# A fallback branch moved from the middle of a recurrence-and-attention kernel to its end, with larger residual fetches and shifted statistics

## The chip, the cores and the metric

The kernel runs on one core of a Trainium2 chip. The metric is the device time of one execution in microseconds (us). Five engines take part: TensorE (PE in the profile), VectorE (DVE), ScalarE (ACT), GpSimd (POOL) and SyncE (SP, which only issues transfers). Each runs its own list of instructions in order, and semaphores make one wait for another.

## The reference, cut to what matters

Everything is float32. `x` has the shape (2, 2048, 256).

```
xi = layernorm(x) @ Wi.T + bi
h_t = tanh(xi_t + h_(t-1) @ Wh.T + bh)          # recurrence over t = 0..2047
x = x + h
y = layernorm(x)
q, k = y @ Wq, y @ Wk                           # 8 heads of 64
wv = top2mask(y @ Ws) * sigmoid(y @ Ws)         # 5 experts per head
v = sum over e of wv[.., e] * (y @ Wv[e])
attn = softmax(q @ k.T / 8) @ v
out = x + sum over h, e of top2mask(y @ Wd) * attn @ Wo[e]
```

The recurrence is sequential over 2048 steps. The kernel does not run it so: it cuts time into 128 segments of 16 steps and treats the segments as columns of one matrix.

## The kernel before, in words

**Recurrence.** `run("a", True, ...)` goes through the steps 3 to 15 of all segments at once, from a zero state, and leaves each segment's last state in `ends`. `run("b", False, ...)` goes through the 16 steps again, each segment starting from its left neighbour's end. If the ends of run b equal those of run a (to a tolerance of four units of 2^-23), the result holds. Beside run b, `beside(s)` turns the states of earlier steps back (`turn_back`, L385), adds them to `x` (`add_back`, L394, which also stores the sum to the DRAM tensor `x1d`), and takes the statistics of the second layer norm of batch 0 (`stats_back`, L399).

**The check and the branch (L503 to L535).** Right behind run b, DVE compares the ends (L505 to L510: four instructions), one matmul sums the count over partitions (`pc`, L515) and DVE writes the integer `again` (L520). `nc.values_load` (L521) makes all five engines read it into a register, and `tc.If(flag > 0)` (L522) branches on it. The body of the branch repeats the recurrence until it must have closed; with the inputs of the test it is skipped. Code on one side of the branch can't be mixed with code on the other.

**Between branch and attention (L537 to L548).** `stats_back(S - 1)`, `roots` (a Newton iteration of small DVE instructions), the normalisation of the second half of batch 0 (`norm_back`, four on DVE and four on POOL), then on PE `queries(0, 0)`, `logits(0)`, `keys(0, 0)`, `logits(4)` and the transposes `turn_norm`.

**Attention.** 16 pairs of batch and head, four blocks of 512 queries each: 64 units. A unit takes four steps T, so T runs from 0 to 255; each step handles two tiles of 256 keys by 512 queries. PE multiplies (`scores`, L636), ACT copies the scores to an SBUF ring (`stage`, L648), DVE keeps a running maximum (`largest`, L658). At the unit's end PE transposes the maximum (`turn_max`), DVE reduces it (`reduce_max`, mq, L682), and PE spreads it again (`spread_max`, pt, L691). Some steps later POOL or DVE subtracts it (L704), ACT takes the exponential (L707), PE multiplies by v (`products`, L717), POOL's transfer queue folds pairs of tiles (`fold`, L729, an accumulating transfer), and PE sums them (`sums`, L738). `close` and `gather` weigh and store a head's output in `yd`; for the last head `fetch_y` (L804) reads it back and POOL adds (L840). `turn_out` (L848) transposes a chunk of 128 rows and fetches its residual `z` from `x1d` (L862, 128 KB, three buffers); `project_out` (L865) multiplies by Wo, DVE adds `z` (L878), SP stores it (L879).

**Order of the work.** Inside `tc.manual_schedule()` every engine takes its instructions in program order. Within a step the order is written out in the loop from L1127; what is not part of the fixed step hangs in the tables `before` (ahead of `products`) and `behind` (at the step's end), filled from L939 to L1025. Batch 1 is normalised there, late: `load_late` (L884), `stats_late` (L888): for each unit from the fourth on, a pair of chunks has both statistics at the end of the unit's last step (L983). `drain` (L1027) is the hand-written order behind the last step: it transposes the last 14 and projects and stores the last 15 of the last batch's 16 chunks while the last two units finish.

**The end.** When the program's last transfers are issued, SP waits for their semaphores and all engines meet (L1223).

Of the kernel before, what the change touches and what calls it, by code (L numbers as in the profile page):

```python
# [8 lines left out]
F32 = mybir.dt.float32  # L9
# [8 lines left out]


@with_exitstack  # L20
def rnn_then_switchhead_kernel(
    ctx: ExitStack,
    tc: tile.TileContext,
    x: bass.AP,
# [8 lines left out]
    Wv: bass.AP,  # L33
    Wo: bass.AP,
    out: bass.AP,
):
    nc = tc.nc
    B, T, D = x.shape
    E, _, DH = Wv.shape
    H = Wq.shape[1] // DH  # L40
# [7 lines left out]
    HE = H * E  # L48
    SCALE = float(DH) ** -0.5

    const = ctx.enter_context(tc.tile_pool(name="const", bufs=1))
    keep = ctx.enter_context(tc.tile_pool(name="keep", bufs=1))
    early = ctx.enter_context(tc.tile_pool(name="early", bufs=1))

    rw = ctx.enter_context(ExitStack())
    rconst = rw.enter_context(tc.tile_pool(name="rconst", bufs=1))
# [4 lines left out]
    dram = ctx.enter_context(tc.tile_pool(name="dram", bufs=1, space=bass.MemoryType.DRAM))  # L63
    x1d = dram.tile([NCH, P, B, D], F32, name="x1d")
    yd = dram.tile([B, T // 512, P, 4, E, DH], F32, name="yd")
    xvd = dram.tile([B, NCH // 4, P, 4, DH, E], F32, name="xvd")

    def load_x(c):
        nc.sync.dma_start(
# [48 lines left out]
    ps_m = ctx.enter_context(tc.tile_pool(name="ps_m", bufs=2, space=PSUM))  # L118

    def misc(shape, nm):  # L120
        return ps_m.tile(shape, F32, tag="m", name=nm)
# [136 lines left out]
    NEWTON = 3  # L258


    rst = rw.enter_context(tc.tile_pool(name="rst", bufs=1))
    xi = rst.tile([P, KC, S, B, NS], F32, name="xi")
    hs = rst.tile([P, KC, S, B, NS], F32, name="hs")

# [2 lines left out]
    nc.gpsimd.memset(ends, 0.0)  # L267
    nc.gpsimd.memset(ones, 1.0)

    with tc.tile_pool(name="prep", bufs=3) as pp, tc.tile_pool(  # L270
        name="lna", bufs=3
    ) as lnp, tc.tile_pool(name="ps_xi", bufs=3, space=PSUM) as ps_xi, tc.tile_pool(
        name="ps_t", bufs=3, space=PSUM
    ) as ps_t, tc.manual_schedule():
        norm_of, turned = {}, {}
# [61 lines left out]

    TOL = 4 * 2.0**-23  # L340
    GC = NCH // 2
    SKIP = 3
    EARLY = S - 1
    sp = rw.enter_context(tc.tile_pool(name="step", bufs=3))
    lnp = rw.enter_context(tc.tile_pool(name="ln", bufs=2))
    ps_t = ctx.enter_context(ExitStack())
    pst = ps_t.enter_context(tc.tile_pool(name="ps_tb", bufs=2, space=PSUM))
    mv2 = [sp.tile([P, GC, 2], F32, tag=f"mv{g}", bufs=1, name=f"mvb{g}") for g in range(2)]
    hv_of, root_of = {}, {}

# [144 lines left out]
                )  # L495
        nc.scalar.copy(gates_all[:, c0 : c0 + 4, 0, :], pg)

    with tc.tile_pool(name="ps_h", bufs=1, space=PSUM) as ps_h:

        with tc.manual_schedule():  # L500
            run("a", True, False, ps_h)
            run("b", False, True, ps_h, beside)
            N = KC * B * NS  # L503
            off = sp.tile([P, KC, B, NS], F32, tag="off", bufs=1, name="off")
            nc.vector.tensor_tensor(off, hs[:, :, S - 1], ends[:, :, :, 1:], ALU.subtract)  # L505
            good = sp.tile([P, KC, B, NS], F32, tag="good", bufs=1, name="good")
            nc.vector.tensor_scalar(good, off, TOL, None, ALU.is_le)
            nc.vector.scalar_tensor_tensor(good, off, -TOL, good, ALU.is_ge, ALU.mult)
            count = sp.tile([P, 1], F32, tag="count", bufs=1, name="count")
            nc.vector.tensor_reduce(count, good.rearrange("p c b n -> p (c b n)"), AX.X, ALU.add)  # L510
            turn_back(S - 1, "b")
            for c in range(0, GC, 2):
                turn_norm(c, xn_of.pop(c), "b")
            pc = misc([1, 1], "pc")
            nc.tensor.matmul(pc, lhsT=count, rhs=ones, start=True, stop=True)  # L515
            for c in (S - 2, S - 1):
                add_back(c, nc.vector)
            stats_back(EARLY - 1, "b")
            again = sp.tile([1, 1], I32, tag="again", bufs=1, name="again")
            nc.vector.tensor_scalar(again, pc, float(P * N) - 0.5, None, ALU.is_lt)  # L520
        flag = nc.values_load(again[0:1, 0:1], min_val=0, max_val=1)  # L521
        with tc.If(flag > 0):  # L522
            for c in range(S):
                load_x(c)
            with tc.For_i(0, NS - 1, 1):
                nc.vector.tensor_copy(ends[:, :, :, 1:], hs[:, :, S - 1])
                run("c", False, True, ps_h)
            for c in range(S):
                turn_back(c, "c")
                add_back(c, nc.gpsimd)  # L530
                if c < EARLY:
                    stats_back(c, "c")
            *_, root_of[0] = roots(mv2[0], GC, "c")
            for c in range(0, GC, 2):
                turn_norm(c, norm_back(c, "c", pool2), "c")  # L535

    with tc.manual_schedule():  # L537

        stats_back(S - 1, "d")
        *_, root_of[1] = roots(mv2[1], GC, "d")  # L540
        for c in range(GC, S, 2):
            xn_of[c] = norm_back(c, "d", (nc.vector, nc.gpsimd))
        queries(0, 0)
        logits(0)
        keys(0, 0)
        logits(4)
        for c in range(GC, S, 2):
            turn_norm(c, xn_of.pop(c), "d")  # L548
# [8 lines left out]
    U_T = NCH // 4  # L557
    LAG = U_T + 2
    RING = (LAG + 4, LAG + 3)
    big = ctx.enter_context(tc.tile_pool(name="big", bufs=1))  # L560
    ap = ctx.enter_context(tc.tile_pool(name="attn", bufs=2))
    four = ctx.enter_context(tc.tile_pool(name="four", bufs=1))
    ps_o = ctx.enter_context(tc.tile_pool(name="ps_o", bufs=1, space=PSUM))
    scores_only = ctx.enter_context(ExitStack())
    ps_s = scores_only.enter_context(tc.tile_pool(name="ps_s", bufs=2, space=PSUM))
# [282 lines left out]
    def turn_out(b, c):  # L848
        yf = y_of[b, c // QS][:, c % QS].rearrange("p e k -> p (e k)")
        py = other(f"py{b}_{c}")[:, : len(o_chunks) * P] if spare else misc([P, len(o_chunks) * P], f"py{b}_{c}")  # L850
        py = py.rearrange("p (k n) -> p k n", n=P)
        for k, (r0, m) in enumerate(o_chunks):
            nc.tensor.transpose(py[0:m, k, :], yf[:, r0 : r0 + m], ident)  # L853
        yT = yT_all[yT_of["n"] % 2]
        yT_of["n"] += 1
        full = sum(m == P for _, m in o_chunks)
        nc.scalar.copy(yT[:, 0:full, :], py[:, 0:full, :])  # L857
        for k, (r0, m) in enumerate(o_chunks):
            if m < P:
                nc.scalar.copy(yT[0:m, k, :], py[0:m, k, :])  # L860
        z = ap.tile([P, D], F32, tag="z", bufs=3, name=f"z{b}_{c}")
        nc.sync.dma_start(out=z, in_=x1d[c, :, b, :])  # L862
        yT_of[b, c] = (yT, z)

    def project_out(b, c, at_end=False):  # L865
        yT, z = yT_of.pop((b, c))
# [69 lines left out]
        late["c"].pop(0)()  # L936


    before, first_behind, behind = {}, {}, {}  # L939

    def at(table, T, f, *a):
        table.setdefault(T, []).append(lambda: f(*a))
# [34 lines left out]
    for b in range(1, B):  # L977

        T0 = (b - 1) * H * H_T + 2 * LAG + 3
        for c in range(NCH):  # L980
            T = T0 + c // 2 * U_T
            at(behind, T - 2 + c % 2, load_late, b, c)
            at(behind, T, stats_late, b, c)  # L983
        T0 += NCH // 2 * U_T
        for part in range(2):
            at(behind, T0 + 3, scales_late, b, part)
            T0 += U_T
        for c in range(NCH):
# [12 lines left out]
        assert T0 <= b * H * H_T  # L1001
# [25 lines left out]
    def drain():  # L1027
# [13 lines left out]
        def project(n=1):  # L1041
            nonlocal projected
            for _ in range(n):
                project_out(*outs[projected])
                projected += 1

        spread_max(v)
        turn_max(u)
        subtract(tv + 6, True)
# [22 lines left out]
        products(tv + 7)  # L1072
        fold(tv + 6)
        turn()
        project()
        take(v)
        sums(tv, tv + 2, True, False)
        exponential(tu + 2)
# [47 lines left out]
    with tc.manual_schedule():  # L1126
        for T in range(NT):  # L1127
# [49 lines left out]
        assert not before and not behind and not first_behind  # L1177
        scores_only.close()
        spare["pool"] = ctx.enter_context(tc.tile_pool(name="ps_z", bufs=4, space=PSUM))
        drain()  # L1180


# [44 lines left out]
```

## Time and profile before

| what | value |
|---|---|
| three runs, median (lowest to highest) | 1567.89 us (1567.87 to 1571.04) |
| the profiled execution itself | 1569.4 us |
| its span, first to last instruction | 1567.6 us |
| mean granted TensorE clock | 0.997 |
| PE busy | 1512.6 us, 96% |
| DVE, POOL, ACT busy | 1299.1, 1287.7, 1247.8 us |

The stages, read from the timeline of each engine: the input side and both runs of the recurrence reach to about 114 us; check, branch and the first projections to about 130 us; attention from there to about 1512 us; the drain to the end. The profile shows, for each group of instructions, where it is in the code, what it writes and reads, how long one takes, and what ended the idle time of its engine before it. "issue" means that the engine waited for nothing that the profile shows. An entry such as PEldq or SPq is an engine's sequencer: waits on semaphores, register loads, branches.

### The profile page before, as it was taken

How to read it: one execution, taken by the hardware profiler on the slowest of the kernel's cores; microseconds unless marked ns; L12 is line 12 of the kernel's file. 1: busy time of each engine (PE TensorE's matmuls, PEld its weight loads, DVE VectorE, ACT ScalarE, POOL GpSimd, SP SyncE). 2: the span in 40 equal slices, each digit the busy share in tenths (PEclk: the TensorE clock that was granted, in tenths of full speed). 3: DMA queues.
4: the chain of work that ended last, by engine and by line, in shares of the span. 5: the costliest groups of instructions: out<-in, count | busy, mean ns of one | idle time of the engine just before them, and what ended most of it. 6: DMA issues, size and time to landing. Idle time of an engine off the chain costs nothing. (4 is left out here: it accounts for less than half of the span.)

```text
span 1567.6 us, 41503 instructions
## 1 busy us (share of the span) xinstructions
PE 1512.6 (96%) x17582; PEld 533.7 (34%) x17582; DVE 1299.1 (83%) x1811; ACT 1247.8 (80%) x1617; POOL 1287.7 (82%) x855
## 2 busy tenths in 40 slices
PE   6988899999999999999999999999999999999997
PEld 5984222222233333333223332222222222222233
DVE  7473799999988888888987779999999999999873
ACT  4674688888888888888887778888888888888882
POOL 3053699898999988999998778899999999999980
PEclk9999999999999999999999999999999999999999
DMA  5021377888889987888897767788888888888955
GB/s 167 1 109 32 102 153 189 186 187 176 181 174 188 177 180 161 173 171 175 171 202 155 163 159 181 170 178 179 176 179 178 176 176 170 176 174 176 197 117 149
DMA packets 86959, 254.09 MB, mean 162 GB/s; under 512 B 11952, under 2 KB 31216, under 8 KB 86768
## 3 DMA queue, kind: packets, MB, share of 16 engines
q0 software_dynamic: 43488, 164.65, 57.5%
q1 hardware_dynamic: 41648, 86.13, 16.5%
q8 instruction: 139, 2.28, 0.6%
q10 hardware_dynamic: 1632, 0.61, 0.1%
q14 instruction: 52, 0.43, 0.1%
HBM read 59.46 MB, written 50.33 MB: 70 GB/s over the span
## 5 line engine op out<-in xcount | busy, mean ns | idle before, releaser
L704 POOL TENSOR_TENSOR p<-p,top 128x1024 f32<-128x1024 f32 x378 | 1006.3, 2768 | 27.9 <-ACT top L697 27.4
L648 ACT COPY p<-s 128x1024 f32<-128x1024 f32 x512 | 511.7, 1013 | 139.8 <-issue 49.5
L707 ACT ACTIVATE p<-p 128x1024 f32<-128x1024 f32 x512 | 538.8, 1063 | 50.7 <-DVE p L704 41.9
L636 PE MATMUL s<-q,k 64*32 64x512 f32 x4096 | 501.6, 596 | 3.6 <-ACT p L648 2.4
L636 PE MATMUL s<-qs,k 64*32 64x512 f32 x4096 | 501.4, 596 | 3.3 <-ACT p L648 1.8
L717 PE MATMUL o<-p,v 128*32 128x512 f32 x4096 | 491.0, 597 | 3.2 <-DVE os L754 2.3
L658 DVE TENSOR_TENSOR m<-s,m 128x1024 f32<-128x1024 f32 x320 | 390.9, 1222 | 89.4 <-PE s L636 80.8
L729 POOL DMA_DIRECT2D p<-p x254 | 263.0, 1036 | 97.6 <-issue 42.4
L717 PEld LDWEIGHTS o<-p,v 128*32 128x32 f32 x4096 | 113.5, 109 | 299.4 <-issue 158.0
L636 PEld LDWEIGHTS s<-qs,k 64*32 64x32 f32 x4096 | 100.3, 105 | 154.6 <-ACT p L648 58.2
L636 PEld LDWEIGHTS s<-q,k 64*32 64x32 f32 x4096 | 100.2, 105 | 153.9 <-ACT p L648 59.9
L704 DVE TENSOR_TENSOR p<-p,pt 128x1024 f32<-128x1024 f32 x126 | 152.5, 1210 | 0.0
L738 PE MATMUL d<-p,ones 128*32 128x512 f32 x1032 | 135.0, 592 | 0.9 <-DMA p<-p 0.9
L658 DVE TENSOR_TENSOR m<-s,p 128x1024 f32<-128x1024 f32 x64 | 78.4, 1225 | 57.5 <-ACT p L648 57.0
L783 DVE TENSOR_TENSOR pro<-po,mr 128x1280 f32<-128x1280 f32 (+1 forms) x67 | 95.9, 1431 | 2.7
L620 DVE TENSOR_TENSOR xq<-xq,wp 128x1280 f32<-128x1280 f32 x60 | 89.2, 1487 | 2.3 <-DVE wp L618 0.2
L626 DVE TENSOR_REDUCE v<-xq 128x256 f32<-128x1280 f32 x60 | 88.5, 1476 | 0.0
L159 PE MATMUL pq<-xn2T,wq 128*32 128x512 f32 x512 | 63.2, 612 | 6.4 <-DVE rtd L427 6.4
L140 PE MATMUL pk<-xn2T,wk 128*32 128x512 f32 x512 | 61.5, 597 | 0.0
L837 POOL DMA_DIRECT2D yd<-pro x48 | 61.0, 1270 | 0.0
L738 PEld LDWEIGHTS d<-p,ones 128*32 128x32 f32 x1032 | 33.9, 110 | 77.8 <-issue 75.8
L396 POOL TENSOR_TENSOR x<-x,hvb 128x512 f32<-128x512 f32 x14 | 17.9, 1276 | 45.8 <-ACT hs L369 34.2
(179 smaller groups left out, 1493.5 us busy)
## 6 DMA issues: line engine op xcount, KB each, us to landing
p<-p POOLq DMA_DIRECT2D x254, 512.0 KB, 5.4
xq<-xvd SPq DMA_DIRECT2D x60, 640.0 KB, 4.6
yd<-pro POOLq DMA_DIRECT2D x48, 640.0 KB, 6.5
qs<-q SPq DMA_DIRECT2D x64, 128.0 KB, 4.5
yd<-pro SPq DMA_DIRECT2D x8, 640.0 KB, 5.9
y<-yd SPq DMA_DIRECT2D x8, 640.0 KB, 7.3
x<-in_x SPq DMA_DIRECT2D x16, 256.0 KB, 5.5
x1d<-x SPq DMA_DIRECT2D x16, 256.0 KB, 2.0
```

The lines of the kernel that those rows point to most:

```text
L159: nc.tensor.matmul(pq[at_col : at_col + 32, :], lhsT=wq[:, kc, h * DH + g : h * DH + g + 32], rhs=xn2T[:, kc, b, n * QB : (n + 1) * QB], s ...
L620: nc.vector.tensor_tensor(xq, xq, wp.unsqueeze(2).to_broadcast([P, 4, DH, E]), ALU.mult)
L626: nc.vector.tensor_reduce(v_of[i][:, 4 * part : 4 * part + 4, :], xq, AX.X, ALU.add)
L636: nc.tensor.matmul(ss[g : g + 32, o, :], lhsT=k_of[i][half, c, g : g + 32], rhs=q_of[i, n][o][half, :], start=True, stop=True, tile_positi ...
L648: nc.scalar.copy(p, ss)
L658: nc.vector.tensor_tensor(m, ss, ring[t - 1] if c == 1 else m, ALU.max)
L704: eng.tensor_tensor(p, p, top.unsqueeze(1).to_broadcast([P, 2, QB]), ALU.subtract)
L707: nc.scalar.activation(ring[t], ring[t], AF.Exp)
L717: nc.tensor.matmul(o_of[u][at_col : at_col + 32, :], lhsT=v_of[i][:, 2 * c + o, g : g + 32], rhs=ring[t][:, o, :], start=c == 0, stop=c == ...
L729: nc.gpsimd.dma_start(out=ring[t], in_=ring.pop(t + 1), accum_op=ALU.add)
L738: nc.tensor.matmul(den_of[u][32 * g : 32 * (g + 1), :], lhsT=ones32, rhs=ring[(t, t1)[g // 2]][:, g % 2, :], start=first, stop=last, tile_ ...
L783: nc.vector.tensor_tensor(dst, po[:, s : s + n, 0:DH].unsqueeze(2).to_broadcast([P, n, E, DH]), mr[:, s : s + n].unsqueeze(3).to_broadcast ...
```

## The change

The whole kernel becomes a function `pass_over(..., again, slow)`. The new `rnn_then_switchhead_kernel` calls it once with `slow=False`, reads the flag at the very end, and has a second complete pass with `slow=True` as the body of the branch. Four further edits are in it:

- The check becomes `compare()` and stands between `keys(0, 0)` and `logits(4)`. Run b is followed at once by the last `turn_back`, `add_back` and `stats_back`, and then, with no branch between, by `turn_norm` and `roots`.
- `stats_late` goes from `behind` to a new table `between`, which the step reads ahead of `largest` of its second tile. The even chunk stays in the unit's last step, the odd one goes to the next step.
- The residuals of the last 12 chunks are fetched by `load_z`, four chunks in one transfer of 512 KB, into buffers of the ring of odd tiles; two of them at the start of the drain and one inside it. `turn_out` fetches no `z` for those chunks.
- In the drain `fetch_y(v)` stands some steps earlier, behind the second `turn()`.

Every pool gets another name in the second pass; that is left out here.

```diff
+    def compare():
+
+        N = KC * B * NS
+        off = sp.tile([P, KC, B, NS], F32, tag="off", bufs=1, name="off")
+        nc.vector.tensor_tensor(off, hs[:, :, S - 1], ends[:, :, :, 1:], ALU.subtract)
...
+        nc.tensor.matmul(pc, lhsT=count, rhs=ones, start=True, stop=True)
+        nc.vector.tensor_scalar(again, pc, float(P * N) - 0.5, None, ALU.is_lt)
+
+    with tile_pool(name="ps_h", bufs=1, space=PSUM) as ps_h:
+        if slow:
...
+        else:
+            with tc.manual_schedule():
+                run("a", True, False, ps_h)
+                run("b", False, True, ps_h, beside)
+                turn_back(S - 1, "b")
+                for c in (S - 2, S - 1):
+                    add_back(c, nc.vector)
+                    stats_back(c, "b")

     with tc.manual_schedule():
-
-        stats_back(S - 1, "d")
+        for c in range(0, GC, 2):
+            turn_norm(c, xn_of.pop(c), "b")
         *_, root_of[1] = roots(mv2[1], GC, "d")
         for c in range(GC, S, 2):
             xn_of[c] = norm_back(c, "d", (nc.vector, nc.gpsimd))
         queries(0, 0)
         logits(0)
         keys(0, 0)
+        if not slow:
+            compare()
         logits(4)
...
-        z = ap.tile([P, D], F32, tag="z", bufs=3, name=f"z{b}_{c}")
-        nc.sync.dma_start(out=z, in_=x1d[c, :, b, :])
+        z = yT_of.pop(("z", b, c), None)
+        if z is None:
+            z = ap.tile([P, D], F32, tag="z", bufs=3, name=f"z{b}_{c}")
+            nc.sync.dma_start(out=z, in_=x1d[c, :, b, :])
         yT_of[b, c] = (yT, z)
+
+    def load_z(b, n):
+
+        z = ap.tile([P, QS, D], F32, tag="p1", bufs=RING[1], name=f"zz{b}_{n}")
+        nc.sync.dma_start(out=z, in_=x1d[n * QS : (n + 1) * QS, :, b, :].rearrange("c p d -> p c d"))
+        for s in range(QS):
+            yT_of["z", b, n * QS + s] = z[:, s, :]
...
-            at(behind, T, stats_late, b, c)
+            at(between, T + c % 2, stats_late, b, c)
...
+        load_z(B - 1, NQ - 3)
+        load_z(B - 1, NQ - 2)
         spread_max(v)
         turn_max(u)
...
         fold(tv + 6)
         turn()
+        fetch_y(v)
         project()
+        load_z(B - 1, NQ - 1)
         take(v)
...
         products(tu + 1)
         turn()
-        fetch_y(v)
         fold(tu)
...
                     reduce_max(T // U_T - 1)
+                for f in between.pop(T, []):
+                    f()
                 largest(new[1], ss[1])
             else:
+                for f in between.pop(T, []):
+                    f()
                 largest(new[1], ss[1])
...
+@with_exitstack
+def rnn_then_switchhead_kernel(ctx: ExitStack, tc: tile.TileContext, *args):
+    nc = tc.nc
+    flags = ctx.enter_context(tc.tile_pool(name="flags", bufs=1))
+    again = flags.tile([1, 1], I32, name="again")
+    pass_over(tc, *args, again, False)
+    flag = nc.values_load(again[0:1, 0:1], min_val=0, max_val=1)
+    with tc.If(flag > 0):
+        pass_over(tc, *args, again, True)
```

More of the change, by code (lines that the diff above doesn't have):

```diff
@@ L20, in rnn_then_switchhead_kernel, with pass_over @@
 @with_exitstack
-def rnn_then_switchhead_kernel(
+def pass_over(
     ctx: ExitStack,
@@ L35, in rnn_then_switchhead_kernel, with tile_pool @@
     out: bass.AP,
+    again: bass.AP,
+    slow: bool,
 ):
     nc = tc.nc
+    tc_pool, mark = tc.tile_pool, "s" if slow else ""
+    def tile_pool(name, **kw):
+        return tc_pool(name=name + mark, **kw)
     B, T, D = x.shape
@@ L49, in rnn_then_switchhead_kernel @@
     SCALE = float(DH) ** -0.5
-    const = ctx.enter_context(tc.tile_pool(name="const", bufs=1))
-    keep = ctx.enter_context(tc.tile_pool(name="keep", bufs=1))
-    early = ctx.enter_context(tc.tile_pool(name="early", bufs=1))
+    const = ctx.enter_context(tile_pool(name="const", bufs=1))
+    keep = ctx.enter_context(tile_pool(name="keep", bufs=1))
+    early = ctx.enter_context(tile_pool(name="early", bufs=1))
     rw = ctx.enter_context(ExitStack())
-    rconst = rw.enter_context(tc.tile_pool(name="rconst", bufs=1))
+    rconst = rw.enter_context(tile_pool(name="rconst", bufs=1))
     xt = []
@@ L62, in rnn_then_switchhead_kernel @@
         xt.append(t)
[L63 to L66, printed above, removed]
+    dram = ctx.enter_context(tile_pool(name="dram", bufs=1, space=bass.MemoryType.DRAM))
+    x1d = dram.tile([NCH, P, B, D], F32, name="x1d" + mark)
+    yd = dram.tile([B, T // 512, P, 4, E, DH], F32, name="yd" + mark)
+    xvd = dram.tile([B, NCH // 4, P, 4, DH, E], F32, name="xvd" + mark)
     def load_x(c):
@@ L116, in rnn_then_switchhead_kernel @@
     gates_all = keep.tile([P, NCH, B, 2 * HE], F32, name="gates_all")
-    ps_m = ctx.enter_context(tc.tile_pool(name="ps_m", bufs=2, space=PSUM))
+    ps_m = ctx.enter_context(tile_pool(name="ps_m", bufs=2, space=PSUM))
     def misc(shape, nm):
@@ L258, in rnn_then_switchhead_kernel @@
     NEWTON = 3
-    rst = rw.enter_context(tc.tile_pool(name="rst", bufs=1))
+    rst = rw.enter_context(tile_pool(name="rst", bufs=1))
     xi = rst.tile([P, KC, S, B, NS], F32, name="xi")
@@ L268, in rnn_then_switchhead_kernel @@
     nc.gpsimd.memset(ones, 1.0)
-    with tc.tile_pool(name="prep", bufs=3) as pp, tc.tile_pool(
+    with tile_pool(name="prep", bufs=3) as pp, tile_pool(
         name="lna", bufs=3
-    ) as lnp, tc.tile_pool(name="ps_xi", bufs=3, space=PSUM) as ps_xi, tc.tile_pool(
+    ) as lnp, tile_pool(name="ps_xi", bufs=3, space=PSUM) as ps_xi, tile_pool(
         name="ps_t", bufs=3, space=PSUM
@@ L342, in rnn_then_switchhead_kernel @@
     SKIP = 3
-    EARLY = S - 1
-    sp = rw.enter_context(tc.tile_pool(name="step", bufs=3))
-    lnp = rw.enter_context(tc.tile_pool(name="ln", bufs=2))
+    sp = rw.enter_context(tile_pool(name="step", bufs=3))
+    lnp = rw.enter_context(tile_pool(name="ln", bufs=2))
     ps_t = ctx.enter_context(ExitStack())
-    pst = ps_t.enter_context(tc.tile_pool(name="ps_tb", bufs=2, space=PSUM))
+    pst = ps_t.enter_context(tile_pool(name="ps_tb", bufs=2, space=PSUM))
     mv2 = [sp.tile([P, GC, 2], F32, tag=f"mv{g}", bufs=1, name=f"mvb{g}") for g in range(2)]
@@ L496, in logits @@
         nc.scalar.copy(gates_all[:, c0 : c0 + 4, 0, :], pg)
[L498 to L525, printed above, removed]
@@ new lines, in compare @@
+    def compare():
+        N = KC * B * NS
+        off = sp.tile([P, KC, B, NS], F32, tag="off", bufs=1, name="off")
+        nc.vector.tensor_tensor(off, hs[:, :, S - 1], ends[:, :, :, 1:], ALU.subtract)
+        good = sp.tile([P, KC, B, NS], F32, tag="good", bufs=1, name="good")
+        nc.vector.tensor_scalar(good, off, TOL, None, ALU.is_le)
+        nc.vector.scalar_tensor_tensor(good, off, -TOL, good, ALU.is_ge, ALU.mult)
+        count = sp.tile([P, 1], F32, tag="count", bufs=1, name="count")
+        nc.vector.tensor_reduce(count, good.rearrange("p c b n -> p (c b n)"), AX.X, ALU.add)
+        pc = misc([1, 1], "pc")
+        nc.tensor.matmul(pc, lhsT=count, rhs=ones, start=True, stop=True)
+        nc.vector.tensor_scalar(again, pc, float(P * N) - 0.5, None, ALU.is_lt)
@@ L526, in rnn_then_switchhead_kernel @@
+    with tile_pool(name="ps_h", bufs=1, space=PSUM) as ps_h:
+        if slow:
+            nc.gpsimd.memset(hs[:, :, S - 1], 0.0)
+            with tc.For_i(0, NS, 1):
                 nc.vector.tensor_copy(ends[:, :, :, 1:], hs[:, :, S - 1])
@@ L530, in rnn_then_switchhead_kernel @@
                 add_back(c, nc.gpsimd)
-                if c < EARLY:
-                    stats_back(c, "c")
+                stats_back(c, "c")
             *_, root_of[0] = roots(mv2[0], GC, "c")
             for c in range(0, GC, 2):
-                turn_norm(c, norm_back(c, "c", pool2), "c")
+                xn_of[c] = norm_back(c, "c", pool2)
+        else:
[6 more added lines that the diff above has]
+                    stats_back(c, "b")
     with tc.manual_schedule():
-        stats_back(S - 1, "d")
+        for c in range(0, GC, 2):
+            turn_norm(c, xn_of.pop(c), "b")
         *_, root_of[1] = roots(mv2[1], GC, "d")
@@ L559, in rnn_then_switchhead_kernel @@
     RING = (LAG + 4, LAG + 3)
[L560 to L563, printed above, removed]
+    big = ctx.enter_context(tile_pool(name="big", bufs=1))
+    ap = ctx.enter_context(tile_pool(name="attn", bufs=2))
+    four = ctx.enter_context(tile_pool(name="four", bufs=1))
+    ps_o = ctx.enter_context(tile_pool(name="ps_o", bufs=1, space=PSUM))
     scores_only = ctx.enter_context(ExitStack())
-    ps_s = scores_only.enter_context(tc.tile_pool(name="ps_s", bufs=2, space=PSUM))
+    ps_s = scores_only.enter_context(tile_pool(name="ps_s", bufs=2, space=PSUM))
     units = [(i, n) for i in range(len(heads)) for n in range(NQ)]
@@ L936, in gates_go_on @@
         late["c"].pop(0)()
-    before, first_behind, behind = {}, {}, {}
+    before, between, first_behind, behind = {}, {}, {}, {}
     def at(table, T, f, *a):
@@ L1176, in rnn_then_switchhead_kernel @@
                 f()
-        assert not before and not behind and not first_behind
+        assert not before and not between and not behind and not first_behind
         scores_only.close()
-        spare["pool"] = ctx.enter_context(tc.tile_pool(name="ps_z", bufs=4, space=PSUM))
+        spare["pool"] = ctx.enter_context(tile_pool(name="ps_z", bufs=4, space=PSUM))
         drain()
+@with_exitstack
[7 more added lines that the diff above has]
+        pass_over(tc, *args, again, True)
 def kernel(
```

## The prediction, on record before the result

> **What bounds the kernel now.** I first read the busy time by window. From 1000 to 1100 us PE is busy 99.61 of 100 us, so in attention only an idle PE can be saved. The gaps between PE's instructions lie in three places, and the change touches each of them.
>
> The waits from 113 to 121 us show the first:
>
> ```profile
> POOL xn2d L213 <- DVE rootd L434: 9.1, 1, 9.1
> PEld pq L159 <- issue: 6.5, 1, 6.5
> DVE stbd L179 <- DVEq L522: 1.8, 1, 1.8
> ```
>
> PE waits 6.5 us for nothing that the profile can name. The instructions of lines 521 and 522 name it:
>
> ```profile
> L521 SPq TENSOR_LOAD <-again x1: 747/747/747, 115.3 to 115.3; - x1
> ...
> L522 DVEq COMPARE_BRANCH  x1: 72/72/72, 116.2 to 116.2; - x1
> L522 PEldq COMPARE_BRANCH  x1: 3872/3872/3872, 116.2 to 116.2; - x1
> ...
> L522 SPq EVENT_SEMAPHORE  x8: 17/17/17, 116.9 to 117.5; - x8
> ```
>
> The same branch takes 0.07 us on DVE and 3.87 us on PE. Behind it PE starts slowly: the 16 matmuls of `queries` take 3.64 us here and 1.92 us later (at 242.81).
>
> The second place, PE's waits from 205 to 385 us:
>
> ```profile
> PE pt L691 <- DVE mq L682: 3.5, 8, 0.7
> ```
>
> Eight units, each with a pair of late statistics; on DVE the pair (1.19 us, 253.09 to 254.29 us) stands ahead of the reduction mq, and PE waits 0.38 us or more for it. Units without the pair have no such wait (none from 1000 to 1400 us).
>
> The third is the drain; DVE's timeline and then PE's:
>
> ```profile
> 1534.50 0.42 DVE L878 TENSOR_TENSOR z<-pz,z 128x256 f32<-128x256 f32 x1 [6.88 <-issue]
> ...
> 1535.65 1.22 DVE L704 TENSOR_TENSOR p<-p,pt__17190 128x1024 f32<-128x1024 f32 x1
> 1538.63 0.42 DVE L878 TENSOR_TENSOR z<-pz,z 128x256 f32<-128x256 f32 x1 [1.76 <-DMA z<-x1d]
> ```
>
> ```profile
> 1539.12 0.65 PE L770 MATMUL po<-ident,os 128*128 128x128 f32 x4 [2.54 <-DVE z L878]
> ...
> 1542.15 1.50 PE L870 MATMUL pz<-wo,yT 128*32 128x256 f32 x24 [0.53 <-DVE den L772]
> ```
>
> DVE stands still for residuals: a 128 KB fetch issued at 1526.95 landed at 1533.7, since SP could issue it only when a buffer was free and two folds were ahead. Behind the waiting addition are a subtraction and the release of PSUM tiles, so PE stops too: 2.54 + 0.53 us, and 0.93 us at 1546.2 for POOL's late addition of y.
>
> [...] one engine of five pays 3.87 us, the one with the longest skipped body, and a 16 KB instruction packet of 1.37 us begins 1.0 us after its branch. [...] The four engines [...] take 45 to 72 ns here. [...] the granted clock from 121 to 131 us is 0.78. [...] The trace shows 1 KB packets of about 53 ns among 4 KB fold packets of 345 ns[...].
>
> **The change part by part.**
>
> *Front.* After run b, DVE is free at 110.7. `add_back(14)` waits for ACT's copy (110.9) and ends at 111.6, its statistics at 112.2; the second addition waits for the copy of 111.87, and with statistics (0.43 + 0.18) ends at 113.4. `roots` took 117.63 to 120.61, 3.0 us: to 116.5. DVE's four normalisations 2.04 us: to 118.6. Then the comparison, which took 110.64 to 113.39, 2.75 us: count at 121.3. PE ends `turn_norm` at 113.9 and ACT copies it until 114.54, so `queries` can start at 114.6, not 120.45. [...] the three groups advance by about 1.8 us each (126.62 to 128.47 for `keys`): 114.6 + 1.8 + 1.85 + 1.85 = 120.1. Now the added wait: the `pc` matmul is queued ahead of `logits(4)` and the transposes, and needs the count of 121.3: 1.2 us idle[...]. Then 0.2 us, `logits(4)` 1.85 us, and the transposes start at 123.3. Before they started at 130.3. **Front: −7.0 us.** Without the compare in PE's queue it would be −8.2; if ACT or POOL were late instead, perhaps −6. DVE's final write of `again` is covered: DVE's next work came 15 us later (137.67). All of attention moves with this.
>
> *Statistics.* No instruction is added. The even chunk now runs ahead of `largest` in the unit's last step, where DVE already waits 0.66 us for PE's scores (248.44): it fits, 0.6 us. The odd one runs behind the reduction, ahead of `largest`, at 254.5 to 255.1, and `largest` began at 255.7 before. So mq comes 1.2 us earlier and the wait for pt goes: 7 × 0.39 + 0.74 = 3.5 us at most, of which I take **−3.1 us** (8 × 0.39). If the loads were late DVE would wait at the new place: an odd one landed at 252.5 against a new use at 254.5, an even one at 237.0 against 247.8. SP's load queue holds the same entries, freed within 0.4 us of the old times.
>
> *Drain.* Twelve fetches of 128 KB become three of 512 KB. The first needs a free buffer of the odd ring at the drain's start, the second that of the fold issued at 1508.8, which landed at 1513.4; so SP issues both by 1514, ahead of the store of 1515.8. The third needs the fold that landed at 1519.1, and stands behind the store of 1522.6. `fetch_y(v)` comes at about 1520.5 (the transpose of chunk 3, which frees its buffer) instead of 1528.2. The extra traffic from 1512 to 1528 is 3 × 512 packets of 53 ns over 16 engines, 5.1 us of the share, where the share was 0.49, 1.04, 0.79 and 0.37 in four-us slices: room enough. The cost is to the folds: [...] 8 fold packets per engine meet 8 small ones, 8 × 53 ns = 0.4 us each; PE used the fold of 1525.27 at 1529.9 with 0.2 us to spare. Bounds: 0 to 2 us, value 0.2.
>
> DVE then runs through: `take_sums` 1532.2, the subtraction to 1533.5, ACT's two exponentials to 1535.6. PE has no gap until 1536.57, takes po at once, products to 1539.0, the projection to 1540.4, the sums to 1543.2. In the meantime DVE's weighing ends at 1539.3 and POOL's 2.95 us at 1542.3, under the sums. That is what is late next, by 0.9 us of slack. The gaps of 2.54 + 0.53 + 0.93 = 4.0 us are gone: PE ends at 1558.9 instead of 1562.9. The last addition waited for its residual until 1564.32; now it follows PE directly and ends at 1559.35 instead of 1564.75. **Drain: −5.4 + 0.2 = −5.2 us.**
>
> *End.* Before, from the end of SP's last issue (1565.1) to the span's end: 2.5 us. Now SP, in order: the register load to its branch 1.14 us (115.27 to 116.41), the branch, eight waits that join the skipped path 0.6 us (116.92 to 117.45), then the list of final waits 0.8 and the meeting 0.8, as now. The skipped body is a whole pass on each engine[...]. The branch costs between 0.07 us and two fetches in a row, 7.7 us; I take the one measured, 3.87 us. Sum 7.2 + 0.05 against 2.5: **+4.8 us**, between +1.0 and +8.6. The last store (1.5 us to land) hides inside. `tc.If` joins only behind it, so nothing else covers this.
>
> **Sum.** −7.0 − 3.1 − 5.2 + 4.8 = −10.5 us. The span of 1567.6 becomes 1557.1; with the 1.8 us around it the profiled execution would go from 1569.4 to 1558.9. Against the median of the three runs, 1.5 us lower than that execution, 1567.89 − 10.5 = **1557.4 us**.
>
> **Rivals.** *A, the end is almost free:* the branch costs 0.07 us, as four engines showed. Against it: those bodies were short. 1557.4 − 3.8 = 1553.6 us. *B, the drain gains nothing:* folds that meet the large fetches, or POOL's addition, take the place of the residual. For it: PE's spare before the fold is 0.2 us, POOL's 0.9. Against: packets and slices above. 1557.4 + 5.2 = 1562.6 us. *C, the comparison delays PE more:* `pc` is 2 us later than worked out and the gap becomes a cold start (1.7 us): 1561.1 us. *D, slower than before:* the closing branch costs more than all gains. Place: the program's end, behind the last store; price: 3.87 us [...]. The gains are 15.3 us and the rest of the end costs about 0.9, so it decides from 14.4 us, four fetches in a row; with five it is 1567.89 − 15.3 + 0.9 + 19.4 = 1572.9 us. [...] Against: PE on its one branch stalled once. That the branch isn't removed can't be: the flag is read after the drain.
>
> **Numbers.** Forecast 0.64 (own range 1554.5 to 1560), A 0.12, B 0.11, C 0.08, D 0.05. The range 1552.5 to 1562.5 holds the forecast, A, C and, with the two-fetch bound of the end, 1561.2; it leaves out D and most of B, under 0.2. A measurement of this kernel can tell about 0.2%, 3.1 us, from no change. Below 1564.75 lie the forecast, A, C and B: faster 0.93, within 0.04, slower 0.03 (the upper part of D).
>
> **What would show it.** Front: `queries` at about 114.6 taking under 2 us, transposes from 123.3, a PE gap of about 1 us at `pc`. Statistics: no wait of pt for mq from 200 to 380 us. Drain: no DVE wait for z behind chunk 3, PE's last matmul about 14 us earlier than before. End: five long COMPARE_BRANCH entries, and about 7 us from SP's last issue to the end. The prediction is wrong if PE's new waits (for `pc`, folds or y) add up to more than 3 us, or if the end is outside 3 to 11 us.

## The result, and the profile after

| | before | after |
|---|---|---|
| median (lowest to highest), six runs each | 1569.11 us (1567.87 to 1571.04) | 1562.24 us (1560.95 to 1563.88) |
| ratio, with its 95% interval | | 0.9956 (0.9943 to 0.9969) |
| the profiled execution, its span | 1569.4, 1567.6 us | 1562.38, 1560.5 us |

The time fell by 6.9 us where 10.5 were forecast. It lies inside the range, close to rival B. The forecast time of 1557.4 us also stood on a median before of 1567.89 us, from three runs; with six it is 1569.11, so 1.2 of the 4.8 us between 1557.4 and 1562.24 are the base, not the change. Step by step, from the two traces:

| step | forecast | read at | before | after | difference |
|---|---|---|---|---|---|
| front | −7.0 | first `pvf` matmul of attention | 140.06 | 133.17 | −6.9 |
| statistics | −3.1 | first `pt` matmul of the drain | 1512.04 | 1501.95 | −10.1, so −3.2 |
| drain | −5.2 | from there to the end of the last addition | 52.70 | 52.80 | +0.1 |
| end | +4.8 | from the end of SP's last issue to the span's end | 2.5 | 5.4 | +2.9 |
| sum | −10.5 | span | 1567.6 | 1560.5 | −7.1 |

**Front.** The wait without a name ahead of `queries` is gone. From the waits of 113 to 121 us of the changed kernel, the same view as before:

```profile
POOL xn2d L220 <- DVE rootd L441: 5.6, 1, 5.6
...
PEld pq L166 <- issue: 0.7, 3, 0.3
```

PE's timeline shows what is late there now:

```profile
114.14 2.66 PE L166 MATMUL pq<-xn2T,wq 128*32 128x512 f32 x16
...
121.29 0.63 PE L642 MATMUL s<-q,k 64*32 64x512 f32 x4 [0.70 <-ACT k L155]
...
122.30 0.19 PE L516 MATMUL pc<-ones,count 128*1 128x1 f32 x2
```

`queries` starts at 114.14, forecast 114.6. The one gap, 0.70 us, stands ahead of the first scores. These had been behind the branch; now they run ahead of `pc`, so they filled the wait that had been worked out for `pc`. In the text of the kernel they stand behind `pc` and the transposes: at this seam PE's order is not that of the text, before the change (first scores at 130.85 us, among the transposes) as after. The transposes start at 124.27, only 6.05 us earlier, but with part of the first scores done; by the first `pvf` the gain is 6.9.

**Statistics.** The list of PE's waits from 200 to 385 us had pt, waiting for mq, at its head. The whole list is now one line:

```profile
PE s L642 <- ACT p L654: 0.6, 2, 0.4
```

**Drain.** DVE still stands still for a residual, and PE behind it. First DVE's timeline, then PE's:

```profile
1509.77 2.34 DVE L710 TENSOR_TENSOR p<-p,pt__16557 128x1024 f32<-128x1024 f32 x2
1516.72 0.42 DVE L893 TENSOR_TENSOR z<-pz,z 128x256 f32<-128x256 f32 x1 [4.61 <-DMA z<-x1d]
1517.18 0.69 DVE L760 TENSOR_TENSOR os<-o,os 64x512 f32<-64x512 f32 x1
```

```profile
1513.63 0.62 PE L744 MATMUL d<-p,ones 128*32 128x512 f32 x2 [1.08 <-DMA p<-p]
...
1518.02 3.27 PE L723 MATMUL o<-p,v 128*32 128x512 f32 x16 [2.03 <-DVE os L760]
1521.21 1.17 PE L859 MATMUL py<-ident,y 128*128 128x128 f32 x6
```

The residual is that of chunk 2, one of those that are still fetched singly. The addition of it stands on DVE ahead of the one that writes `os` from the finished product `o`, and PE can start the next `o` only behind that. Three losses follow each other: PE waits 1.08 us for a fold, 2.03 us because DVE waits for the residual, and then `o` takes 3.27 us instead of the 1.90 us of the same 16 matmuls at 1523.89: the granted clock is 0.81 from 1516 to 1520 us and 0.77 in the four us behind. The transfers of 1500 to 1520 us point to a cause, which runs 1 to 5 test; first by queue (packets, MB, share of the 16 engines), then by issue (KB each, median us to landing):

```profile
q0 software_dynamic: 573, 2.09, 54.4%
q1 hardware_dynamic: 2122, 2.55, 40.0%
...
zz<-x1d SPq DMA_DIRECT2D x3, 512.0 KB, 5.1
p<-p POOLq DMA_DIRECT2D x3, 512.0 KB, 9.6
y<-yd SPq DMA_DIRECT2D x1, 640.0 KB, 8.2
...
z<-x1d SPq DMA_DIRECT2D x3, 128.0 KB, 9.5
```

The two queues together fill 94% of the engines' time. The single residual issued at 1506.06 landed 10.6 us later; the single fetches of this stretch had needed at most 7.4 us before. Two folds issued at 1504.0 and 1506.7 us landed after 9.6 and 9.7 us; the same two had taken 5.3 and 7.6 us before the change. The old gaps of 2.54, 0.53 and 0.93 us are gone, and the new ones with the low clock cost as much in this profile.

**End.** The register load and the branch of the changed kernel:

```profile
L1212 SPq TENSOR_LOAD <-again x1: 473/473/473, 122.7 to 122.7; - x1
```

```profile
L1213 SPq EVENT_SEMAPHORE  x8: 17/17/17, 1558.3 to 1558.8; - x8
L1213 POOLq EVENT_SEMAPHORE  x5: 17/43/43, 1538.2 to 1538.5; - x5
L1213 POOLq COMPARE_BRANCH  x1: 45/45/45, 1535.6 to 1535.6; - x1
...
L1213 ACTq COMPARE_BRANCH  x1: 50/50/50, 1552.2 to 1552.2; - x1
L1213 PEldq COMPARE_BRANCH  x1: 4140/4140/4140, 1553.4 to 1553.4; - x1
L1213 DVEq COMPARE_BRANCH  x1: 72/72/72, 1555.0 to 1555.0; - x1
L1213 ACTq EVENT_SEMAPHORE  x1: 17/17/17, 1555.1 to 1555.1; - x1
L1213 SPq COMPARE_BRANCH  x1: 53/53/53, 1555.2 to 1555.2; - x1
L1213 PEldq EVENT_SEMAPHORE  x1: 51/51/51, 1557.6 to 1557.6; - x1
L1213 DVEq EVENT_SEMAPHORE  x1: 21/21/21, 1558.4 to 1558.4; - x1
```

SP read the flag at 122.7 us, not at the end: that load is off the path. PE's branch is recorded with 4.14 us. Those of the other four are recorded with 0.05 to 0.07 us, yet the next entry comes 2.6 (POOL) to 3.4 us (DVE) after their start: it looks like the same stall, as silence behind the branch. Each engine branches when its own list ends, POOL already at 1535.6 us; SP is the last, so its 3.1 us are exposed. Between PE's branch and 1558.3 us the trace holds five instruction packets, the first of 16 KB at 1554.4 us, 1.05 us after that branch; run 12 will show the same place without any.

### The profile page after: what moved, and what is told of

Its sections match the earlier page's. It is cut to its first block, busy times and chain, and to the rows that moved or that the text cites. A ratio compares the mean times of both kernels' runs of the same rounds, so it can differ in the third digit from the quotient of the medians.

```text
span 1560.5 us, 41474 instructions
## 1 busy us (share of the span) xinstructions
PE 1513.2 (97%) x17582; PEld 534.4 (34%) x17582; DVE 1300.0 (83%) x1811; ACT 1245.4 (80%) x1617; POOL 1287.0 (82%) x855
## 4 chain that ended last, share of the span: by engine, by line
PE 63%; DVE 19%; ACT 7%; issue 5%; DMA 3%; POOL 1%; ACTq 0%; SPq 0%; DVEq 0%; POOLq 0%
PE s L642 21%; PE o L723 17%; DVE m L664 11%; ACT p L654 5%; PE d L744 4%; DVE pro L789 3%; PE pq L166 3%; PE pk L147 3%; PE pz L885 2%; PE phb L368 2%; PE px L309 1%; PE pha L368 1%; DMA p<-p 1%; DMA z<-x1d 1%; ACT p L713 1%
```

## The experiments

Each has five to nine executions, measured beside the kernel before on the same chip in four groups: 1 to 4, 5 to 8, 9 to 11, and 12 alone. Two columns are from the one trace of each: from the first `pt` matmul of the drain to PE's last matmul, and to the end of DVE's last addition. The ratio is to the kernel before of the same group.

Six of these traces have the drain of the changed kernel: after, 4, 7, 9, 10 and 12. PE's end lies between 49.74 and 52.31 us in them, the last addition between 50.23 and 52.80. A difference of single traces counts only where it leaves this spread.

| run | median us | ratio (95%) | to PE's end | to the last addition |
|---|---|---|---|---|
| before, first profile | 1569.11 | | 50.86 | 52.70 |
| after, first profile | 1562.24 | 0.9956 (0.9943 to 0.9969) | 52.31 | 52.80 |
| 1, all residuals single | 1561.98 | 0.9949 (0.9935 to 0.9962) | 47.99 | 51.38 |
| 2, first two large fetches later | 1562.14 | 0.9955 (0.9941 to 0.9968) | 52.28 | 52.77 |
| 3, large fetches on ACT's queue | 1560.62 | 0.9941 (0.9928 to 0.9955) | 49.99 | 50.48 |
| 4, no branch at the end | 1559.39 | 0.9933 (0.9919 to 0.9947) | 51.87 | 52.36 |
| 5, large fetches spread out | 1558.32 | 0.9925 (0.9911 to 0.9938) | 47.06 | 47.55 |
| 6, old drain | 1565.81 | 0.9965 (0.9951 to 0.9978) | 52.93 | 56.63 |
| 7, statistics behind | 1565.44 | 0.9972 (0.9962 to 0.9982) | 50.45 | 50.94 |
| 8, only the last eight large, late | 1560.90 | 0.9940 (0.9926 to 0.9954) | 49.11 | 49.60 |
| 9, the changed kernel again | 1560.49 | 0.9944 (0.9929 to 0.9959) | 49.74 | 50.23 |
| 10, short body of the branch | 1557.63 | 0.9924 (0.9910 to 0.9939) | 50.25 | 50.74 |
| 11, spread out, comparison later | 1557.25 | 0.9920 (0.9906 to 0.9934) | 47.51 | 47.99 |
| 12, short body, kept at the end | 1557.18 | 0.9921 (0.9908 to 0.9935) | 49.95 | 50.44 |

**1: all residuals single, `fetch_y(v)` stays early.**

```diff
-        load_z(B - 1, NQ - 3)
-        load_z(B - 1, NQ - 2)
...
-        load_z(B - 1, NQ - 1)
```

> The changed kernel without its three large residual fetches: every chunk's residual is fetched alone, as before the change; fetch_y(v) stays early. Theory ring (the single fetches of chunks 2 and 3 stand behind 1 MB of large fetches in SP's own queue): chunk 2's residual lands within 6 us instead of 10.6, DVE's wait of 4.6 us ahead of it and PE's gaps of 1.1 and 2.0 us go, but waits for the residuals of chunks 4 to 7 come back: 1560 to 1563 us, about 0 to 2 us below the changed kernel. Theory bandwidth (the moved traffic itself slows folds and fetches): the same. Theory hidden (the residuals never set the drain's end): within 1 us of the changed kernel, with DVE's wait gone.

Without the large fetches PE ends 47.99 us after the first `pt`, 1.8 to 4.3 us sooner than in the six traces with them, and its waits for a fold and for `os` are gone: it is they that hold the drain's first half up. `fetch_y(v)` is still early here, so it does not do it alone. But the single ones cost the end, as DVE's timeline shows:

```profile
1549.37 0.42 DVE L893 TENSOR_TENSOR z<-pz,z 128x256 f32<-128x256 f32 x1 [2.41 <-DMA z<-x1d]
1552.65 0.42 DVE L893 TENSOR_TENSOR z<-pz,z 128x256 f32<-128x256 f32 x1 [2.85 <-DMA z<-x1d]
```

So the large fetches do remove waits for single residuals, as the prediction said, and pay for it ahead of them.

**2: the first two large fetches behind the second turn and `fetch_y(v)`.**

```diff
-        load_z(B - 1, NQ - 3)
-        load_z(B - 1, NQ - 2)
         spread_max(v)
...
         fetch_y(v)
+        load_z(B - 1, NQ - 3)
+        load_z(B - 1, NQ - 2)
         project()
         load_z(B - 1, NQ - 1)
```

> The changed kernel with the first two large fetches issued behind the fetches of chunks 2 and 3 and behind fetch_y(v), not at the drain's start. Theory ring: chunk 2's residual lands within 6 us, DVE waits for no residual, PE's last matmul about 5 us earlier than in the changed kernel counted from the drain's start, 1557 us. Theory bandwidth: the folds still meet 1 MB of small packets, a stall of 2 to 4 us stays, 1560 to 1562 us.

No residual is waited for any more, and nothing is won, since the load only meets later folds. From PE's timeline:

```profile
1519.66 1.03 PE L744 MATMUL d<-p,ones 128*32 128x512 f32 x4
1523.87 1.71 PE L744 MATMUL d<-p,ones 128*32 128x512 f32 x4 [3.18 <-DMA p<-p]
```

A wait on a residual became one on a fold. That speaks for the traffic as a whole and against the order of one queue alone.

**3: the large fetches issued by ACT.**

```diff
-        nc.sync.dma_start(out=z, in_=x1d[n * QS : (n + 1) * QS, :, b, :].rearrange("c p d -> p c d"))
+        nc.scalar.dma_start(out=z, in_=x1d[n * QS : (n + 1) * QS, :, b, :].rearrange("c p d -> p c d"))
```

> The changed kernel with the three large fetches issued at the same places but by ACT's queue instead of SP's. The bytes and the moments stay; only the queue differs. Theory ring: chunk 2's residual, now alone in SP's queue, lands within 7 us, DVE's wait of 4.6 us falls under 1 us, 1557 to 1559 us. Theory bandwidth: chunk 2's residual still takes about 10 us and the time stays at 1562 us. [...]

The slowest residual lands after 8.4 us, where the six traces with all fetches on SP's queue have 9.6 to 10.6; DVE waits 2.6 us for it instead of 3.7 to 4.6, and no fold is waited for. So a share of the delay, 1 to 2 us, goes with the large fetches' place in SP's queue. The rest stays on another queue too: PE still waits 2.0 us for `os`, and neither its end (49.99 us) nor the median leaves the spread of the changed kernel, so no gain in time is shown.

**4: no register load, no branch, no second pass.** The recurrence's fallback is left out.

> The changed kernel without the register load, the branch and the second pass; the comparison is still computed but nothing is done with it, so the fallback is left out. Theory exposed (the closing branch stalls every engine for about 3 us behind the last store): the stretch from SP's last issue to the end falls from 5.3 to 2.5 us, 1559.4 us. Theory hidden (the last store and the final waits cover it): unchanged, 1562.2 us.

From SP's last issue (1555.1) to the end it is 2.6 us, nearly as before the change (2.5), instead of 5.4: the closing branch costs 2.8 us. The ratio agrees (1.7 to 3.6 us below the changed kernel's two measurements, first and ninth run).

**5: the large fetches spread out.**

```diff
-        load_z(B - 1, NQ - 3)
-        load_z(B - 1, NQ - 2)
...
+        load_z(B - 1, NQ - 3)
         fetch_y(v)
         project()
-        load_z(B - 1, NQ - 1)
...
         fold(tu + 2)
+        load_z(B - 1, NQ - 2)
...
         fetch_y(u)
+        load_z(B - 1, NQ - 1)
```

> The first large fetch goes behind the second turn of the drain, the other two behind fold(tu + 2) and fetch_y(u), after the last fold. Traffic theory (the large fetches and the folds hold each other up while both are in flight from 1504 to 1516): no fold and no residual is waited for, PE's gaps in the drain add up to under 1 us, PE ends about 47.5 us after the drain's first pt matmul instead of 52.3 and the time is about 1557.5 us (1556.5 to 1559). Rival, the drain is bound by another chain (POOL's subtractions, ACT's exponentials, the release of PSUM tiles): a gap of another name takes the place, PE ends 51 us or later and the time stays at 1561 to 1563 us.

This is the decisive run. The list of PE's waits from 1498 to 1556 us is one line, where the changed kernel has `os` with 2.0 us and the fold with 1.1 us:

```profile
PE pz L885 <- ACT yT L863: 0.5, 2, 0.3
```

The drain is 5.2 us shorter than in the profile before the change, 4.7 in run 11 with the same drain; the prediction gave the edit 5.2. Only the places of the fetches differ from the changed kernel. All five executions (1556.50 to 1558.77 us) are shorter than each of the twelve of the changed kernel (from 1559.14 us on). The transfer engines are not emptier (share 1.01 to 1.09 from 1508 to 1528 us, 0.90 to 1.06 in the changed kernel from 1500 to 1524); but what is needed next is no longer behind what is needed 20 us later: the slowest single residual lands after 7.3 us, where it took 10.6 behind two large fetches that were issued at 1502.9 us and first added at 1524.1.

**6: the drain as before the change, all else changed.** The edit of run 1, and `fetch_y(v)` back behind the third turn.

> The drain exactly as before the change (single fetches, fetch_y(v) at its old place), all else as changed. If the drain's edits gave and cost about the same: 1561 to 1563 us, DVE waiting for residuals and PE's gaps of 2.5 + 0.5 + 0.9 us as before, and the last addition 52 to 53 us after the first pt matmul. If the edits gained their 5 us, and something that moved with the front took it away again: 1566 to 1568 us.

It is 0.1 to 0.2% slower than the changed kernel (1.4 and 3.3 us against its two measurements), between the two expectations; the intervals overlap. Its five runs spread from 1561.83 to 1566.78 us, and the profile is of the longest. There the old wait is longer and is followed by slow matmuls, which the profile of before does not have:

```profile
1526.94 1.50 PE L885 MATMUL pz<-wo,yT 128*32 128x256 f32 x24 [1.56 <-DVE z L893]
1531.52 1.07 PE L776 MATMUL po<-ident,os 128*128 128x128 f32 x4 [3.07 <-DVE z L893]
1532.52 3.14 PE L723 MATMUL o<-p,v 128*32 128x512 f32 x16
```

So the drain's edits are worth some 1 to 3 us as they stand, if they are told apart at all, and 52.70 us for the old drain was one draw of several.

**7: statistics back behind the step.**

```diff
-            at(between, T + c % 2, stats_late, b, c)
+            at(behind, T, stats_late, b, c)
```

> The late statistics back behind the step, all else as changed. Theory: eight waits of pt for mq of about 0.4 us come back, 3.1 us, so 1565.3 us (1564 to 1566.5). Rival, the move only shifts the wait to the largest of the next tile: under 1 us, 1562.2 to 1563.2 us.

PE's waits from 200 to 385 us are led by pt again:

```profile
PE pt L697 <- DVE mq L688: 5.0, 8, 1.5
```

2.5 and 4.4 us slower than the changed kernel's two measurements. The forecast's 3.1 lies between. Why these eight waits sum to 5.0 us, and to 3.5 before, is not shown.

**8: only the last eight residuals large, both fetches after the last fold.** As run 5, without its first `load_z`; chunks 4 to 7 are single.

> Chunks 4 to 7 fetched singly as before the change, only the last eight in large fetches, both after the last fold; fetch_y(v) at its new place. Traffic theory: no large fetch meets a fold, PE ends about 47.7 us after the first pt matmul as with all single ones, and the last addition follows it within 1 us instead of 3.4 us: about 1558 us (1557 to 1560). Rival, the late fetches hold up the last stores or the last gathered y as much as the singles' own waits did: 1561 to 1563 us.

About half of the gain at most came: 0.6 and 2.5 us below the changed kernel's two measurements, and against the ninth run the intervals nearly coincide. No fold is waited for, but the singles of chunks 4 to 7 are, and POOL's addition of y shows:

```profile
PE py L859 <- POOL y L846: 0.9, 1, 0.9
PE po L776 <- DVE z L893: 0.7, 1, 0.7
```

The first large fetch is worth having, if it stands where run 5 has it: all of run 5's executions are shorter than all of these (from 1559.82 us on).

**9: the changed kernel again.**

> The changed kernel itself, beside the two others of this call on one chip: 1561.5 to 1563 us, a PE gap at a fold and one at os in the drain as in the first profile, since the transfers are issued in the same order.

The median is 1.75 us lower, and the drain of this profile 2.6 us shorter. The transfers are issued in the same order; the wait for the fold is 0.27 us instead of 1.08, and the wait for `os` (1.91 us) is followed by `o` at full speed, 1.92 us. The low clock comes in some executions only. The six traces with this drain, in us:

| trace | wait for the fold | wait for `os` | the 16 `o` behind it | to PE's end |
|---|---|---|---|---|
| after | 1.08 | 2.03 | 3.27 | 52.31 |
| 4 | 0.56 | 2.12 | 3.28 | 51.87 |
| 7 | 0.85 | 2.04 | 1.92 | 50.45 |
| 10 | 0.73 | 1.96 | 1.92 | 50.25 |
| 12 | 0.42 | 1.97 | 1.92 | 49.95 |
| 9 | 0.27 | 1.91 | 1.92 | 49.74 |

Runs 4 and 10 show how near the two cases lie. The rows of 1516 to 1520 us, the granted clock behind the sums of the five engines; first run 4, then run 10:

```profile
1516.00:1520.00 4.00, 2.04 (x12) 0.72 (x16) 3.27 (x4) 0.90 (x1) 0.39 (x1) 0.80 0.83 168
```

```profile
1516.00:1520.00 4.00, 2.09 (x18) 0.73 (x19) 3.32 (x4) 0.95 (x1) 0.78 (x2) 1.00 0.84 173
```

Run 4 had waited 0.56 and 2.12 us, run 10 0.73 and 1.96 us: 2.7 us each, and run 4's PE ends 1.6 us later after the first `pt`. Run 7 waited 2.9 us and kept its clock, so the length of the waits does not decide alone; what does is not shown. The longest single wait ahead of the low clock in these six traces is 2.12 us.

**10: the branch over one memset.**

```diff
-        pass_over(tc, *args, again, True)
+        nc.gpsimd.memset(again, 0)
```

> The second pass, the body of the closing branch, is replaced by one memset on POOL; register load, branch and final waits stay. If the end is paid to the fetch of instructions behind a long skipped body: the stall of about 3 us goes, from SP's last issue to the end about 2.6 to 3 us instead of 5.3, and the time is 2.3 to 2.7 us below the changed kernel's, at about 1559.7 us. If it is paid to the register load, the branch itself and the joining of engines: about 5 us stay and the time is that of the changed kernel.

The fallback is left out here. Inconclusive on the end. With a body that depends on nothing late the branch was placed at 123 to 140 us on every engine, so the end is that of run 4, 2.6 us, and 2.9 us of time are gone. It shows one thing: PE's branch over a short body took 0.23 us.

**11: run 5 with the comparison behind the last transposes.**

```diff
-        if not slow:
-            compare()
         logits(4)
         for c in range(GC, S, 2):
             turn_norm(c, xn_of.pop(c), "d")
+        if not slow:
+            compare()
```

> The spread fetches together with the comparison moved behind the last transposes. Theory: PE's wait at the count's matmul (0.7 us) goes too, the first attention step comes 0.7 us earlier, and the time is 0.5 to 0.9 us below that of the spread fetches alone, 1557.6 us, or 5 us below the changed kernel's of this call. Rival: the wait only moves, since the first scores ran ahead of the count anyway: the same as the spread fetches alone, 1558.3 us.

PE's gap of 0.70 us is gone, and from the second group of the earlier transposes (112.2 us) to the first `pvf` it is 20.0 us instead of the 21.0 of run 9. In the time it can't be told apart from run 5 (0.9920 against 0.9925); in this profile PE's gaps between 800 and 850 us sum to 1.68 us, where run 9 has 0.50 and the first profile of the changed kernel 1.05.

**12: the branch over one transfer that depends on the last stores.** The second pass is left out.

```diff
-        pass_over(tc, *args, again, True)
+        x, out = args[0], args[-1]
+        nc.sync.dma_start(out=out, in_=x)
```

> The second pass is left out: the closing branch skips a single transfer from x to out, which depends on the last stores and so keeps the branch at the end on all five engines; register load, branch, joining waits and final waits stay. If the stall is the fetch of instructions behind a long skipped body: PE's COMPARE_BRANCH takes under 0.3 us as in the run before with the branch in mid-program, the silence of about 3 us behind SP's and DVE's branches goes, from SP's last issue to the end 2.6 to 3.4 us instead of 5.3, and the time is about 1559.5 us. If the stall belongs to any branch that all engines take at the end: 5.3 us and 1560.5 to 1562.2 us stay.

The branch stands at the end on all five engines, and the stall is gone:

```profile
L1213 PEldq COMPARE_BRANCH  x1: 236/236/236, 1551.1 to 1551.1; - x1
...
L1213 SPq COMPARE_BRANCH  x1: 53/53/53, 1552.9 to 1552.9; - x1
L1213 SPq EVENT_SEMAPHORE  x1: 17/17/17, 1553.0 to 1553.0; - x1
```

SP goes on 0.2 us after its branch instead of 3.1, its last issue is 2.6 us from the end, and no instruction packet starts behind PE's branch. The 2.8 us of the closing branch go with the whole pass that it skips: with one transfer as its body the branch, the flag and the meeting of the engines are all still there, and the end takes the 2.6 us of run 4, which has no branch. The packets that are there with the long body and not with the short one speak for a fetch of instructions as the reason, which is not shown beyond that. The median is lower than expected by 2.3 us; the drain of this profile is 2.4 us shorter than that of the first, as in run 9.

## Why the prediction was right or wrong

**Front, −7.0: right**, measured −6.9. The mechanism was the one named: the branch, and the slow start behind it, are gone from PE's path. No run puts the branch back there alone, so this rests on the two traces. That it hit to a tenth is in part luck, for two details failed and cancelled: `queries` took 2.66 us, not under 2 (full speed there was the author's estimate and held, with a granted clock of 1.00, so that is not the reason), and the wait of 1.2 us for the count at `pc` was filled by scores, which the working had left behind `pc`; PE waited 0.70 us for ACT's copy of k instead.

**Statistics, −3.1: right**, measured −3.2 in the traces, and 2.5 to 4.4 us when undone alone (run 7).

**Drain, −5.2: wrong as written, +0.1 in the first profile** and −0.3 to −2.5 in the five others with the same drain. The residual waits that the step removes were priced about rightly: run 5 gains 5.2, run 11 4.7. The failed step is "room enough" with its "value 0.2" for the folds. Its own numbers said otherwise: the four shares sum to 2.69, that is 10.8 of 16 us taken, and 5.1 us more make 15.9 of 16. On top came `fetch_y(v)`, which the step moved into this stretch and did not add: 640 KB, by estimate 2.8 us at the 233 GB/s of 1500 to 1520 us. That is 18.7 us of transfers for 16. Fullness alone does not decide, since run 5 has it too (a share of 1.01 to 1.09 from 1508 to 1528 us) and PE waits for no transfer there; what differs there is what is queued ahead of the next thing needed.

The 0.4 us for each fold was an estimate, 53 ns for each of 8 small packets, one to each of a fold's packets on an engine; that the two meet so was not shown, and it was too small by far: the two folds that met the large fetches landed 4.3 and 2.1 us later than before. Most of that was slack, so the bound of 2 us held for PE's wait (1.08 us). But the residuals of chunks 2 and 3, still single, were not on the list of those that wait; DVE's 4.61 us are chunk 2's. And the price of a gap was taken as its length, though the low clock that can follow it cost 1.6 us more (run 4 against run 10). Run 1 removes the large fetches and the waits go, run 2 moves them and the wait moves to a fold, run 3 takes another queue and the residual lands 1 to 2 us sooner, run 5 spreads them and PE waits for neither.

The prediction's own signs did not catch this. PE's new waits for `pc`, folds and y sum to 1.1 us, under its limit of 3; the 2.03 us for `os` and the 0.70 us for k were not on that list. PE's last matmul shows it: it came 8.6 us earlier, not 14.

This was rival B, with its mechanism half right: the folds did meet the large fetches, but the residual went on being the later one, and of the changed kernels POOL's addition of y mattered only in run 8.

**End, +4.8: right in direction, too high by 1.9 us.** Two terms of the sum were mis-sized. The register load to the branch, 1.14 us, is 0 on the path, because SP read the flag at 122.7 us. The branch, taken at PE's 3.87 us, is SP's 3.1 us. The joining waits (0.6) and the rest (1.6) came as written. That the whole pass may cost something on every engine fits the trace: all five go silent behind their branch, for 2.6 to 4.14 us, none waits for another's stall, and only the last one, SP's, is exposed. The bound of two fetches in a row, and the four and five of rival D, were multiples of the one 3.87 us, an estimate; the changed kernel's trace holds no stall of such a length. Rivals A and D are both excluded. But "five long COMPARE_BRANCH entries" was wrong, for four of them are short with silence behind.

**The sum.** The drain missed by 5.3 us and the end by −1.9; the first two steps miss by a tenth each, in opposite directions. That is the difference between −10.5 and −7.1. That the result was inside the range is luck: B's time was near its edge and the end was cheaper, while the forecast's sum did not hold. The second measurement of the changed kernel (−8.8 us) is nearer, as its drain is 2.6 us shorter.

The best version tried that keeps the fallback is that of runs 5 and 11: 1557 to 1558 us, 3 to 6 us below the changed kernel. Not tried: those drains with a shorter fallback.

## What to carry to other kernels

When a change brings transfers forward, add up all that then lies in the same stretch, moved ones too, as time of the transfer engines against the stretch's length. Where the sum comes near that length (94% of it here, in the two queues), the question is no longer what fits but what is queued ahead of the next thing needed, so issue large fetches that are needed late after the small ones that are needed next (here the drain became 4.7 to 5.2 us shorter than before the change, in runs 11 and 5). Price a gap of the bounding engine with the low clock that can follow it (here 1.6 us, in two traces of six), and expect the time to vary from run to run (1559.14 to 1563.88 us in twelve executions of the changed kernel). A fallback at a program's end cost 2.8 us here with a whole pass as its body, and nothing that shows with a single transfer (2.6 us from SP's last issue to the end, as without the branch).

## What the runs showed of the hardware that was not expected

- The stall behind the branch over a whole pass is in the recorded duration of the branch on PE (3.90 to 4.16 us in the changed kernel and runs 5, 9 and 11) and not on the other engines: there the branch shows 45 to 72 ns, and in the changed kernel the next entry of the engine comes 2.6 to 3.4 us later. The stalls began at 1535.6 us on POOL and at 1552.2 to 1555.2 us on the other four, each behind the engine's own branch, and of them only SP's, the last, lay open at the end.
- With the same instructions and equal waits, 2.7 us in two parts, the granted clock of the next four us was 0.80 in one execution (run 4) and 1.00 in another (run 10); the 16 matmuls `o` then take 3.3 or 1.9 us. No single wait was longer than 2.12 us.
- Of three 128 KB fetches issued within 6 us, the one ahead of two 512 KB fetches landed after 2.6 us, the two behind them after 10.6 and 9.5 us, on a queue that took only 40% of the engines' time from 1500 to 1520 us.
